# Two more queues in program order, and fillers in alternate units, in the attention of an encoder kernel

## The chip, the cores and the metric

The kernel runs on one core of a Trainium2 chip. The time is device microseconds of one execution. A core has engines that run side by side, each with its own in-order instruction queue: TensorE (PE, with its weight loads shown as PEld), VectorE (DVE), ScalarE (ACT), GpSimd (POOL) and SyncE (SP). In this kernel SP issues only DMA transfers, and POOL issues DMA transfers besides its elementwise work. An instruction waits on its queue until what it needs is done, and what stands behind it on that queue waits too.

## The reference, cut to what matters

The input x is 4 batches of 2048 tokens of 256 features, all in float32. The first part of the network is a dense attention with 16 heads of 16 features, a prior added to the scores and a residual:

```python
x = x + attn(layernorm(x))          # this part is "the attention" below
x = x + ffn(layernorm(x))           # two layers of local attention and gated MLP

def attn(x):
    Q, K, V = heads(x @ Wq.T + bq), heads(x @ Wk.T + bk), heads(x @ Wv.T + bv)
    scores = Q @ K^T / sqrt(16) + prior_lambda * gaussian_mask
    out = softmax(scores) @ V
    return merge(out) @ Wo.T + bo
```

For each of 64 pairs of batch and head, a 2048 x 2048 matrix of scores is made, its row maxima are taken, it is exponentiated and multiplied with V. The second part has two layers; its code is called "the local layers" here.

## The kernel before, in words

**Units.** The attention is one loop over t (line 1062 and on in the kernel before), from 0 to 1047. A unit u is 128 tokens of one head, so 16 units make a head, 256 a batch, 1024 the whole. Each turn of the loop does a first pass on unit t and a second pass on unit t − 20 (`LEAD` = 20). The first pass computes the scores of 128 queries against all keys and takes their row maxima (four products, line L775, read by DVE in L787, L789 and L799 and by ACT in L795). The second pass computes the scores again, transposed, with the negative row maxima as extra rows of the operand (four products, L858), adds the prior in the diagonal band (DVE, L869), exponentiates (ACT, L873) and multiplies with V (eight products, L882).

**The row of maxima.** At the end of a head, `negated` (L803 and on) turns its maxima into a row on DVE (L807 to L818). SP stores the row to DRAM (L820) and loads it back, rearranged, into the operand `q2` of the second pass (L824). The second pass of that head needs it about three units later, at units 4, 20, 36 and so on. SP also loads the pieces of q and k for both passes (L708), which are due some units later.

**Fillers.** The rest of the attention is cut into generators, which a timetable runs between the steps of the loop, in two slots per unit (`fill`, called at steps F and E). A filler that wants a product on PE asks `on_pe` first, which lets one filler product through per unit:

```python
def on_pe():
    while phase["at"] is not None and (phase["at"] or phase["taken"]):
        yield 1
    phase["taken"] = True
```

The fillers are: `projections(b)`, which normalises x of the next batch (`normed`, which loads x on POOL's queue) and computes q, k, v of it, with sends from SP to DRAM (L577) of parts made on POOL (L583, L584); `prepare_layers`, which splits the weights and tables of the local layers (loads and stores by SP, L239; POOL's work at L253, L255 and L317); and `residual(b)`. The projections of batch b start 60 units (`PROJECT_AT`) into batch b − 1; the residual of batch b starts 23 units into batch b + 1.

**The residual.** `residual(b)` transposes the attention's output (`oT`, eight fillers), and then goes through four groups g of 512 tokens. For each group, `fetch(g)` loads x (L453) and adds bo to it on POOL (L928); two products with Wo follow (`ao`), which DVE adds to x (L978); the sum is stored (L982); then its statistics are taken on DVE (bn_stats, L987), one of four per unit, with `var` and `nmean` (L991, L994); POOL computes `rstd` (L992) and the normalised `f` (four operations, L1003) and stores it (L1007). For batches 0 to 2, `fetch(0)` stands before the loop and `fetch(g)` at the head of group g; all these DMAs are on POOL's queue. For the last batch, at the end of attention, they are on SP's queue, and `fetch(g + 2)` stands at the end of group g.

**The order.** The attention is written out in the order in which it is to run, and a `manual_schedule` block makes PE, ACT and DVE take that order. In the kernel before, SP and POOL are not in that set: their queues are put in order by a scheduler, apart from the instructions wrapped in `keep_in_program_order`. The local layers follow after the attention with an order of their own, which the change does not touch.

## Time and profile before

| | |
|---|---|
| time, median of 3 | 5775.2 us (5774.78 to 5780.23) |
| the profiled execution | 5777.33 us, of which the span of the profile 5775.5 us |
| PE, DVE, ACT, POOL busy | 5472.3, 4821.5, 4477.9, 2187.8 us |
| mean granted TensorE clock | 0.985 of full |
| attention | from 78 to 3091 us; the last residual to about 3125 us |
| local layers | from there to the end |

The page shows the span in 40 slices with each engine's busy share in tenths, and the clock that TensorE was granted:

```profile
PE   5999999999999999999997899999999999999998
PEld 3444444444444444444444787888787788888787
DVE  5888999879998789999995888888888788888886
ACT  1888998879988799989996677667666666667765
POOL 2232112331012300010002565666665666666665
PEclk7999999999999999999998999999999999999999
```

A slice is 144 us. The attention is the first 21 slices and some, the local layers the rest; between them one slice is less busy. Names such as L775 are lines of the kernel; `s<-k,q` names what an instruction writes and reads. A bracket such as `[4.52 <-DMA x<-in_x]` is idle time of the engine ahead of the instruction, and what ended it. SPq is SP's queue, where only issuing is seen.

### The profile page before, as it was taken

What the parts mean: (1) busy time and instruction counts of PE and PEld (TensorE: products, weight loads), DVE (VectorE), ACT (ScalarE), POOL (GpSimd) and SP (SyncE); (2) the same over time, 40 slices, a digit from 0 to 9 for tenths busy, and PEclk for the clock granted to TensorE, in tenths of its full rate; (3) what the DMA queues carried; (4) which work ended last, traced back from release to release, by engine and by line L of the source; (5) the groups of instructions that cost most, each with busy time, mean ns of one, the idle gap of its engine ahead of it and who ended that gap; (6) DMA issues with size and microseconds to landing.
All of it is one profiled execution on the core that took longest, in us unless ns stands there. A gap on an engine that the chain in (4) does not pass through costs nothing.

```text
span 5775.5 us, 105276 instructions
## 1 busy us (share of the span) xinstructions
PE 5472.3 (95%) x35544; PEld 3386.2 (59%) x35544; DVE 4821.5 (83%) x13779; ACT 4477.9 (78%) x9384; POOL 2187.8 (38%) x2364
## 2 busy tenths in 40 slices
PE   5999999999999999999997899999999999999998
PEld 3444444444444444444444787888787788888787
DVE  5888999879998789999995888888888788888886
ACT  1888998879988799989996677667666666667765
POOL 2232112331012300010002565666665666666665
PEclk7999999999999999999998999999999999999999
DMA  4454234442234522232213212221223222222221
GB/s 128 144 163 118 80 101 135 149 132 82 74 90 123 156 71 62 76 100 61 61 54 110 51 48 55 51 55 51 56 51 84 82 62 58 60 60 55 64 53 40
DMA packets 336841, 477.29 MB, mean 83 GB/s; under 512 B 67376, under 2 KB 191280, under 8 KB 334768
## 3 DMA queue, kind: packets, MB, share of 16 engines
q1 hardware_dynamic: 322480, 432.79, 25.9%
q0 software_dynamic: 13824, 37.78, 2.3%
q8 instruction: 284, 4.65, 0.3%
q14 instruction: 253, 2.07, 0.1%
HBM read 268.79 MB, written 126.09 MB: 68 GB/s over the span
## 4 chain that ended last, share of the span: by engine, by line
PE 56%; DVE 23%; ACT 9%; POOL 6%; issue 3%; DMA 3%; SPq 0%; POOLq 0%; DVEq 0%; ACTq 0%
PE s L775 16%; PE acc L882 15%; PE s L858 8%; PE w L407 4%; ACT sim L1353 4%; PE sim L1327 3%; POOL rn L376 3%; DVE s L789 3%; PE qkv L407 2%; DVE lk L1189 2%; PE po L1407 2%; DVE sim L1339 2%; DVE tops L787 2%; DVE hn L1472 2%; DVE lq L1189 1%
## 5 line engine op out<-in xcount | busy, mean ns | idle before, releaser
L873 ACT ACTIVATE e<-s 128x512 f32<-128x512 f32 x4096 | 2157.9, 614 | 197.9 <-PE s L858 138.4
L775 PE MATMUL s<-k,q 64*128 64x512 f32 x3200 | 1294.7, 467 | 74.3 <-DMA q<-sm 27.2
L789 DVE CUSTOM_DVE_ANT_0 s<-s,wide 128x512 f32<-128x512 f32 x1408 | 973.3, 694 | 185.5 <-PE s L775 175.1
L882 PE MATMUL acc<-e,v 128*32 128x512 f32 x8192 | 1094.2, 606 | 0.3
L858 PE MATMUL s<-q,k 64*128 64x512 f32 x4096 | 841.7, 418 | 29.4 <-DMA q<-rowd 12.6
L775 PEld LDWEIGHTS s<-k,q 64*128 64x128 f32 x3200 | 535.6, 186 | 522.0 <-ACT more L795 257.6
L1353 ACT ACTIVATE sim<-sim,top,rn 128x256 f32<-128x256 f32 (+1 forms) x1024 | 600.6, 590 | 261.3 <-DVE top L1345 253.1
L787 DVE TENSOR_REDUCE tops<-s 128x1 f32<-128x512 f32 x896 | 611.9, 683 | 80.8 <-PE s L775 74.1
L1364 POOL TENSOR_TENSOR sim<-sim,inv 128x512 f32<-128x512 f32 (+1 forms) x512 | 512.8, 1022 | 347.9 <-DVE inv L1361 347.8
L858 PEld LDWEIGHTS s<-q,k 64*128 64x128 f32 x4096 | 542.3, 186 | 163.8 <-ACT e L873 57.3
L795 ACT ACTIVATE more<-s 128x512 f32<-128x512 f32 x896 | 541.3, 604 | 116.9 <-PE s L775 84.0
L799 DVE CUSTOM_DVE_ANT_0 more<-s,more 128x512 f32<-128x512 f32 x896 | 614.0, 685 | 0.0
L775 PEld LDWEIGHTS s<-kd,q 64*128 64x128 f32 x896 | 165.5, 185 | 743.9 <-DVE tops L789 382.6
L869 DVE TENSOR_TENSOR s<-s,band 128x187 f32<-128x187 f32 (+2 forms) x1408 | 474.7, 355 | 90.2 <-PE s L858 89.7
L407 PE MATMUL w<-gt,ww 128*128 128x512 f32 x2112 | 544.9, 397 | 3.5 <-DVE lk L1189 3.1
L775 PE MATMUL s<-kd,q 64*128 64x512 f32 x896 | 447.1, 499 | 1.2 <-DVE tops L787 0.5
L407 PEld LDWEIGHTS w<-gt,ww 128*128 128x128 f32 x2112 | 386.9, 189 | 79.1 <-issue 3.7
L1339 DVE CUSTOM_DVE_ANT_0 sim<-sim,cst 128x256 f32<-128x256 f32 (+1 forms) x1024 | 376.6, 409 | 57.5 <-PE sim L1327 54.0
L1252 POOL TENSOR_TENSOR r<-r,t 128x256 f32<-128x256 f32 x512 | 366.8, 737 | 149.7 <-DVE t L1239 140.0
L376 POOL TENSOR_TENSOR rn<-ss,nhalf 128x16 f32<-128x16 f32 x128 | 372.7, 2912 | 96.5 <-DVE ss L375 93.6
L1327 PE MATMUL sim<-lk,lq 128*128 128x256 f32 (+1 forms) x2048 | 340.8, 296 | 27.7 <-DVE lq L1189 19.1
L1386 PE MATMUL pT<-cst,sim 128*128 128x128 f32 x1984 | 280.7, 278 | 75.4 <-DVE lk L1189 34.2
(173 smaller groups left out, 9416.5 us busy)
## 6 DMA issues: line engine op xcount, KB each, us to landing
lk<-lk SPq DMA_DIRECT2D x256, 256.0 KB
sm<-part SPq DMA_DIRECT2D x192, 256.0 KB
q<-sm SPq DMA_DIRECT2D x512, 96.0 KB
k<-sm SPq DMA_DIRECT2D x512, 96.0 KB
k<-sm SPq DMA_DIRECT2D x128, 192.0 KB
q<-sm SPq DMA_DIRECT2D x128, 192.0 KB
fg<-f SPq DMA_DIRECT2D x32, 512.0 KB
tb<-td SPq DMA_DIRECT2D x128, 128.0 KB
```

The costliest lines, as they stand in the source:

```text
L376: nc.gpsimd.tensor_tensor(dst, var, nhalf[:, : var.shape[1]], ALU.pow)
L407: nc.tensor.matmul(ps, a, c, start=first and k == 0 and i == 0, stop=last and k == n - 1 and i == 2,)
L775: nc.tensor.matmul(ps, q1[u // 4 % Q_BUFS][rows, u % 4 * P : (u % 4 + 1) * P], keys, start=True, stop=True,)
L787: nc.vector.tensor_reduce(top, ps, AX.X, ALU.max)
L789: nc.vector.tensor_tensor_reduce(ps, ps, prior, 1.0, LOWEST, ALU.add, ALU.max, top)
L795: nc.scalar.activation(more, pairs.pop((u, 1, half)), AF.Relu)
L799: nc.vector.tensor_tensor_reduce(more, ps, more, 1.0, LOWEST, ALU.add, ALU.max, tops[u // NC][:, chunk(u), 2 * half : 2 * half + 1],)
L858: nc.tensor.matmul(ps, k2[s // 4 % Q_BUFS][rows, kc % 4 * P : (kc % 4 + 1) * P], q2[h % 2][rows, j % 2 * QT : (j % 2 + 1) * QT], start=Tru ...
L873: nc.scalar.activation(e, sums.pop((s, j)), AF.Exp)
L882: nc.tensor.matmul(acc[32 * j : 32 * j + 32, :], vs[b, kc][:, own * VS : own * VS + 32], es_.pop((s, j)), start=kc == 0, stop=kc == NC - 1,)
L1327: nc.tensor.matmul(ps[:, par, :width], q[:, par, pair, :], kst[:, par, part, windows, pair, :], start=part == 0, stop=part == 1,)
L1353: nc.scalar.activation(w, w, AF.Exp, bias=m["top"][:, h : h + 1], scale=s["rn"][:, h : h + 1], accum_out=m["sums"][:, h : h + 1],)
```

## The change

Three things change, all in the attention.

1. The `manual_schedule` block names all five engines, so SP's and POOL's queues are also in the order in which the program is written. The `keep_in_program_order` wrappers on the way, which then say nothing new, are removed.
2. `fill` marks PE as taken in every odd unit after `LEAD`, so a filler product is let through in even units only, one in two units.
3. `PROJECT_AT` goes from 60 to 90: the projections of batch b start 30 units later in batch b − 1.

Each engine executes the same instructions as before. With fillers in alternate units, the projections of a batch take about 100 units (units 90 to 196 of the batch before) where they took 68 (60 to 127), and a group of the residual takes 8 units where it took 6.

```diff
+ALL_ENGINES = tuple(
+    getattr(mybir.EngineType, name) for name in ("PE", "Activation", "DVE", "Pool", "SP")
+)
...
-PROJECT_AT, STRIDE, XT_BUFS = 60, 1, 4
+PROJECT_AT, STRIDE, XT_BUFS = 90, 1, 4
...
         def load(dst, src):
-            tc.keep_in_program_order(nc.sync.dma_start(dst, src))
+            nc.sync.dma_start(dst, src)
...
-            tc.keep_in_program_order(nc.gpsimd.tensor_copy(h, s))
-            tc.keep_in_program_order(
-                nc.gpsimd.tensor_tensor(low, s, h.bitcast(F32), ALU.subtract)
-            )
+            nc.gpsimd.tensor_copy(h, s)
+            nc.gpsimd.tensor_tensor(low, s, h.bitcast(F32), ALU.subtract)
...
                 def fetch(g):
                     t = x1s_[g] = load_x(b, g, queue, apart_by_four)
-                    tc.keep_in_program_order(
-                        nc.gpsimd.tensor_tensor(
-                            t, t, bo_sb.unsqueeze(1).to_broadcast([P, 4, D]), ALU.add
-                        )
+                    nc.gpsimd.tensor_tensor(
+                        t, t, bo_sb.unsqueeze(1).to_broadcast([P, 4, D]), ALU.add
                     )
...
             def fill(t, at):
-                phase["at"], phase["taken"] = at, False
+
+                phase["at"], phase["taken"] = at, t > LEAD and t % 2 == 1
                 fillers.run(2 * t + at + 1)

-            es.enter_context(tc.manual_schedule(engines={mybir.EngineType.PE, mybir.EngineType.Activation, mybir.EngineType.DVE}))
+            es.enter_context(tc.manual_schedule(engines=set(ALL_ENGINES)))
             for t in range(total + LEAD + 4):
```

The wrapper around the table products of `prepare_layers` (L317) goes in the same way.

More of the change, by code (lines that the diff above doesn't have):

```diff
@@ L315, in prepare_layers @@
                         cols = slice(h * half, (h + 1) * half)
-                        tc.keep_in_program_order(
-                            nc.gpsimd.tensor_tensor(
-                                tb[:, :, i : i + 2, cols], rot[:, :, i : i + 2, :],
-                                sc[:, i // 2, cols].unsqueeze(1).unsqueeze(1).to_broadcast(
-                                    [P, 2, 2, half]
-                                ),
-                                ALU.mult,
-                            )
+                        nc.gpsimd.tensor_tensor(
+                            tb[:, :, i : i + 2, cols], rot[:, :, i : i + 2, :],
+                            sc[:, i // 2, cols].unsqueeze(1).unsqueeze(1).to_broadcast(
+                                [P, 2, 2, half]
+                            ),
+                            ALU.mult,
                         )
@@ L926, in fetch @@
                     t = x1s_[g] = load_x(b, g, queue, apart_by_four)
-                    tc.keep_in_program_order(
-                        nc.gpsimd.tensor_tensor(
-                            t, t, bo_sb.unsqueeze(1).to_broadcast([P, 4, D]), ALU.add
-                        )
+                    nc.gpsimd.tensor_tensor(
+                        t, t, bo_sb.unsqueeze(1).to_broadcast([P, 4, D]), ALU.add
                     )
```

## The prediction

> **What bounds the kernel now.** I read the page's busy rows first, then the busy time by window, then the excess of each attention unit over a plain one, and last the chain and the queues where that excess sits. TensorE bounds everything:

> ```profile
> PE 5472.3 (95%) x35544; PEld 3386.2 (59%) x35544; DVE 4821.5 (83%) x13779; ACT 4477.9 (78%) x9384; POOL 2187.8 (38%) x2364
> ```

> In the windows below, the columns after start and end are the length, then busy us and instructions of PE, PEld, DVE, ACT and POOL, the clock, the DMA share and GB/s:

> ```profile
> 1500.00:1700.00 200.00, 198.62 (x1223) 83.31 (x1216) 182.94 (x539) 187.40 (x367) 4.14 (x10) 1.00 0.25 72
> 2700.00:2900.00 200.00, 198.48 (x1216) 82.08 (x1214) 183.40 (x549) 191.06 (x375) 4.00 (x10) 1.00 0.22 63
> 1253.00:1273.00 20.00, 11.83 (x60) 4.79 (x56) 9.12 (x28) 9.45 (x20) 0.76 (x11) 0.74 0.49 148
> 2005.00:2025.00 20.00, 7.98 (x48) 3.83 (x48) 6.50 (x20) 7.42 (x16) 3.81 (x6) 0.71 0.73 213
> ```

> The first window is an undisturbed stretch of attention: PE busy 198.6 of 200 us. A unit issues 16 products without fillers, so 1216 of them are 76 units, 2.63 us each with the end of each head in it (2.60 to 2.61 without). There, only less PE work or nothing at all can help. The two 20 us windows differ: PE stands 8.2 and 12.0 us. Stepping through the starts of all units, I find such holes at four: unit 124 (473 us, 5.1 us over a plain unit and its filler), 132 (502 us, 4.6), 388 (1256 us, 10.2) and 644 (2010 us, 13.6), together 33.5 us. The nine `ao` units of three residuals that follow a normalisation are 0.96 to 1.23 long, 9.6 in all. Unit 21 is 3.4 long (147 us), in the fill of the pipeline, and I leave it alone. The rest of the excess is some 0.5 to 0.75 per head, ordinary work.

> The third hole, on SP's timeline (start, length, engine, line, operation):

> ```profile
> 1252.84 0.40 SPq L708 DMA_DIRECT2D k<-sm  x1
> 1253.34 0.40 SPq L675 DMA_DIRECT2D sv<-vst  x1
> 1253.83 3.75 SPq L708 DMA_DIRECT2D q<-sm  x2
> 1257.63 1.39 SPq L708 DMA_DIRECT2D k<-sm  x3
> 1259.14 0.35 SPq L820 DMA_DIRECT2D rowd<-row  x1
> 1262.38 1.32 SPq L824 DMA_DIRECT2D q<-rowd  x2
> ```

> and in the chain of waits of the same stretch (start, length, what):

> ```profile
> 1257.00 7.53 issue
> ```

> The first score product of a head's second pass needs its row of maxima (L820 out, L824 back in). DVE had that row at about 1248; SP sends it at 1259.14, behind pieces of k and q and a store of v that nobody needed soon. PE starts 2.15 after L824 began, at 1264.53. At 2010 the same place is `q<-rowd` at 2017.39, behind a copy of local-layer weights; at 502 the row store at 498.48; at 473 POOL itself stood 4.44 on `s_rot` ahead of `full` and `part`.

> **The change part by part.** All durations are from the profiled execution: span 5775.5, run 5777.3, 2.1 above the median of 5775.2. I make the sum against 5777.3 and take 2.1 off at the end. Every engine keeps the same instructions; only order and waits move.

> *The four holes, −33.5.* With SP in program order the row store comes right after the negated maxima, ahead of the head's k and kd loads; the only things before it at 388 are three sends of a `part` that POOL was given two units (5.2 us) earlier. The route of a row takes 5.4 us (1259.14 to 1264.53) and the program leaves three units and more, 8 to 9 us. Weight copies of the local layers move to their own place behind attention, and POOL's wait on `s_rot` comes three slots later by the program's own spacing. Ends: 0 if SP's new waits delay the row as much, −33.5; I take the whole, because the route has 3 us to spare.

> *The residual's x, +48.6 +6 −9.6.* This is the cost I see. Before, the scheduler pulled the load of x for the next group forward on POOL's queue, where it could:

> ```profile
> 947.45 1.04 POOL L992 TENSOR_TENSOR rstd_f<-var_f,nhalf 128x4 f32<-128x4 f32 x1 [8.71 <-DVE nmeanf L994]
> 948.61 2.17 POOL L1003 TENSOR_SCALAR f<-x,nmeanf,rstd_f 128x256 f32<-128x256 f32 x4
> 951.07 0.82 POOL L1007 DMA_DIRECT2D f<-f  x1 [0.30 <-POOL f L1003]
> 951.89 0.77 POOL L453 DMA_DIRECT2D x<-in_x  x1
> 957.17 2.38 POOL L928 TENSOR_TENSOR x<-x,bo_sb 128x1024 f32<-128x1024 f32 x1 [4.52 <-DMA x<-in_x]
> ```

> Here L453 fetches a group ahead of its use (the sum L978 of that group ran at about 967). In program order, `fetch(g)` for g = 1, 2, 3 stands behind group g−1's `rstd_f`, four `f` and the store of `f`, and DVE's sum L978 of the same group g stands two units after `nmeanf` of g−1. From the end of `nmeanf` (947.44) to the end of L928 (959.55) is 12.1 us on POOL and its queue. Before, `nmeanf` to the next L978 was 3.1 us (950.54) at one unit's distance; one unit more makes 5.7. So L978 waits 6.4, and behind it on DVE stand all maxima and band sums of the unit, and behind those PE, which owns three banks for the first products. I take 1.0 off for what PE can do meanwhile: 5.4 for each of nine (three groups, batches 0 to 2), 48.6. Ends: the x loads landed in 4.2 to 8.5 us (median 5.3); the fast end with 2.0 off for a PE lead gives 3.3 each, 30; the slow end gives 9.6 each, 86. The middle follows the row that shows this very load. Group 0's load comes behind the last oT, with 0.8 issue, 5.3 landing and 2.4 for L928, 8.5 in all, against about 5.5 until its L978: 2 each after the same discount, 6 for three (ends 0 and 15). The 9.6 of the `ao` units are the present end of this very path and lie inside these stalls, so they come off.

> The trace has this wait once already, at the end of attention, where a load was fetched as late:

> ```profile
> 3114.27 1.28 DVE L978 TENSOR_TENSOR x<-x,ao 128x512 f32<-128x512 f32 x2 [6.77 <-POOL x L928]
> ```

> [...] The measured row is 5.3 us from issue to landing for 512 KB. [...]

> *The projections' x, +3.* Their load is followed by two units until bn_stats, about 6.5 us with a filler; issue 0.8 and landing 5.3 make 6.1. POOL is nearly idle (4 of 200 us) and may be early. Twelve loads: ends 0, and 2 each or 25 with slow landings; near the low end as the median fits.

> *The passage to the local layers, +5.* There SP issues the batch-3 loads, and in program order the load of group 2 follows the store of `f` of group 0 and of group 1's sum, group 3's that of group 1's `f`. Before, the last load left at 3116.60 and PE then stood 15.52 for L978. I put it some 4 to 7 later; ends 0 and +10.

> *Fillers in every other unit, 0.* A filler product costs PE its own length (q/k product 1.30 over a plain unit, `ao` 1.32, transposes 0.72) wherever it stands, as PE is full in plain units. Cover: ACT (191 of 200) and DVE (183) get 1.3 us of PE time to do the evacuation. Ends −4 and +5, from the 0.35 per bn_stats unit that the residual and projections have now.

> *Projections from unit 90, 0.* They then end at about 196 of 256; the next batch's first keys and rows are fetched some 20 units before 256, so 40 units (104 us) remain. If that cover failed, PE would stand for what is missing.

> *Waits that stay.* SP waits 821.5 us for PE before L708 and POOL 891.6 before the memset L767; in program order the things behind them are due later, so I price these at nothing.

> Sum: 5777.3 −33.5 +48.6 +6 −9.6 +3 +5 = 5796.8, less 2.1: **5795 us**.

> **Rivals.**
> 1. *The x loads stay hidden* (ends faster). PE's lead in PSUM or an early POOL covers the nine stalls. For it: the forecast turns at 3.2 us per load (33.5+9.6−6−3−5 over nine), close to my low end of 3.3. Against it: the 6.77 wait above. With none of them: 5775.2 −33.5 +5 = 5747.
> 2. *Slow landings.* Loads meet sends and weight loads, 8.5 instead of 5.3: 3.2 more each, 29 on nine: 5824. The DMA share in the residual's window is 0.55 against 0.22 in quiet ones, which speaks for some of it.
> 3. *The row stalls come back.* A send that waits for POOL blocks SP, and the row store behind it: nothing of the 33.5 is won, 5828. Against: the send's `part` is two units old.
> 4. *The two sides cancel*, each x stall near 3: within 0.2% of before, which is 11.5 us and about what a measurement of this kernel can tell from no change.

> **How the numbers follow.** Forecast with stalls of 3.5 to 7.5 each 0.57 (own range 5778 to 5814); hidden 0.20 (5747 to 5765); slow landings 0.10; row stalls back 0.08; cancelled 0.05. The range leaves out the lowest and highest tenth: 5752 to 5826. Faster 0.20 from the hidden case; same 0.12, from the cancelled case and the forecast's low edge; slower 0.68.

> **What the changed profile would show.** Right: SP's L820 within 1 us of the row at every head, no 7 us "issue" in the chain, and the holes at 1256 and 2010 gone; in its place DVE's sum of x and `ao` waiting for POOL's sum of x and bo, nine times 5 to 7 us in three groups, with POOL waiting for x behind the store of `f`; PE short by the same time in those windows. Wrong: few such waits, or these waits with PE still busy; or rows still late.

## The result and the profile after

The changed kernel takes 5873.5 us (median of 4, 5871.7 to 5876.1) against 5777.7 for the kernel before (median of 4): a ratio of 1.0166, 95% interval 1.0148 to 1.0183, 96 us slower. I forecast slower, but 5795 and no more than 5826.

Line numbers of the kernel after are two to four lower in the attention: L775 is L773, L858 is L856, L882 is L880, L978 is L974, L928 is L925, L453 is L451, L820 is L818. First the page's busy times, then windows of 20 and more us (start and end, length, busy us and instructions of PE, PEld, DVE, ACT and POOL, the clock, the DMA share, GB/s), all of the kernel after:

```profile
PE 5494.3 (94%) x35544; PEld 3400.0 (58%) x35544; DVE 4822.1 (82%) x13779; ACT 4470.8 (76%) x9384; POOL 2184.9 (37%) x2364
```

```profile
1255.00:1275.00 20.00, 20.00 (x126) 9.42 (x126) 15.44 (x47) 17.14 (x35) 4.56 (x9) 1.00 0.72 210
980.00:1000.00 20.00, 13.87 (x79) 7.44 (x77) 9.86 (x28) 7.94 (x15) 4.80 (x5) 0.74 0.38 116
2060.00:2085.00 25.00, 15.06 (x80) 6.16 (x79) 12.59 (x42) 12.07 (x25) 4.60 (x7) 0.74 0.38 106
```

The stretch around 1256, where PE stood 8 us before, is now full: 20.00 of 20. At each of the 64 heads SP now sends the row of maxima (L818) 0.03 us after DVE has it; before, the worst row, ready at 1249.20, left 9.94 us later. New holes stand at 980 to 1000 (a residual) and at 2060 to 2085 (projections). PE's busy time rose by 22 us with the same number of instructions, so some of its products became slower.

The waits, sorted, say the same (engine, what waited, for what: us in total, times, longest):

```profile
PEld s L773 <- DVE tops L787: 517.8, 615, 10.7
DVE x L974 <- POOL x L925: 101.7, 14, 9.1
POOL x L925 <- DMA x<-in_x: 76.8, 14, 9.4
```

In the kernel before, DVE waited for that sum of POOL twice, 12.6 us in all, both behind the attention.

**The balance.** I stepped through the starts of all 1024 units in both traces and took off a plain unit (2.605 us) and the fillers' products; "excess" below is what is left of a unit. The spans differ by 95.2 us (5870.7 − 5775.5):

| | us |
|---|---|
| first 20 units, the filling of the pipeline (unit 20 starts at 138.3, was 144.8) | −6.5 |
| the four row holes (units 124, 132, 388, 644) | −33.5 |
| nine waits for x in groups 1 to 3 of the residuals, 7.6 to 9.4 each | +75.5 |
| three waits for x in group 0, 5.4 to 5.9 each | +16.8 |
| projections: units 140 to 142, 193, 401 to 402, 653 to 654 | +31.8 |
| from the last unit to the first qkv of the local layers (88.9, was 80.3) | +8.6 |
| local layers (2650.1 both) | 0 |
| small differences in the other units | +2.5 |

One wait of the residual, on three engines of the kernel after; first POOL:

```profile
976.61 1.04 POOL L988 TENSOR_TENSOR rstd_f<-var_f,nhalf 128x4 f32<-128x4 f32 x1 [8.79 <-DVE nmeanf L990]
977.77 2.16 POOL L999 TENSOR_SCALAR f<-x,nmeanf,rstd_f 128x256 f32<-128x256 f32 x4
980.23 0.82 POOL L1003 DMA_DIRECT2D f<-f  x1 [0.30 <-POOL f L999]
981.05 0.77 POOL L451 DMA_DIRECT2D x<-in_x  x1
986.48 2.34 POOL L925 TENSOR_TENSOR x<-x,bo_sb 128x1024 f32<-128x1024 f32 x1 [4.67 <-DMA x<-in_x]
```

then DVE, whose sum stands on the queue ahead of the next maxima:

```profile
988.85 0.69 DVE L974 TENSOR_TENSOR x<-x,ao 128x512 f32<-128x512 f32 x1 [6.74 <-POOL x L925]
```

then PE:

```profile
982.99 1.06 PE L880 MATMUL acc<-e,v 128*32 128x512 f32 x8
983.99 0.49 PE L773 MATMUL s<-kd,q 64*128 64x512 f32 x1
990.62 0.79 PE L773 MATMUL s<-k,q 64*128 64x512 f32 x1 [6.13 <-DVE tops L785]
990.62 1.64 PE L856 MATMUL s<-q,k 64*128 64x512 f32 x4
992.61 1.93 PE L880 MATMUL acc<-e,v 128*32 128x512 f32 x8
```

This is the step the prediction described: the load of x behind `rstd`, `f` and the store of `f`, 12.2 us from the end of DVE's `nmeanf` to the end of the sum with bo; DVE waits 6.74; PE has 0.6 us of lead and waits 6.13. What it lacked is in the last two rows: after the wait, four L856 take 1.64 us and eight L880 take 1.93, against 1.06 for the eight before it. The granted clock of that window is 0.74; it is 0.50 from 986.76 to 997.00 and 1.00 around that.

A wait of the projections, POOL first and then DVE:

```profile
2066.05 0.61 POOL L581 CAST partd<-full 128x512 fp32r<-128x512 f32 x1 [8.84 <-DMA sd<-partd]
2066.74 1.28 POOL L582 TENSOR_TENSOR partd<-full,partd 128x512 fp32r<-128x512 f32 x1
2067.95 1.21 POOL L575 DMA_DIRECT2D sd<-partd  x2
2069.59 0.60 POOL L575 DMA_DIRECT2D sd<-partd  x1 [0.43 <-issue]
2070.17 0.82 POOL L451 DMA_DIRECT2D x<-in_x  x1
```

```profile
2077.41 0.43 DVE L538 BATCH_NORM_STATS2 st_a<-x 128x6 f32<-128x256 f32 x1 [10.85 <-DMA x<-in_x]
```

The x load of the next projection group stands behind the differences of keys. The second of these needs a `part` buffer that the first store must release, so POOL waits 8.84 us for that DMA; the load goes out only then, and bn_stats waits 10.85 us with everything of DVE behind it.

### The profile page after: what moved, and what is told of

It reads as the page before. It is cut to its first block, busy times and chain, and to the rows that moved or that the text cites. A ratio compares the mean times of both kernels' runs of the same rounds, so it can differ in the third digit from the quotient of the medians.

```text
span 5870.7 us, 105058 instructions
## 1 busy us (share of the span) xinstructions
PE 5494.3 (94%) x35544; PEld 3400.0 (58%) x35544; DVE 4822.1 (82%) x13779; ACT 4470.8 (76%) x9384; POOL 2184.9 (37%) x2364
## 4 chain that ended last, share of the span: by engine, by line
PE 23%; DVE 16%; ACT 8%; POOL 5%; issue 2%; DMA 1%; POOLq 0%; DVEq 0%; SPq 0%; ACTq 0%
PE w L405 4%; ACT sim L1350 4%; PE acc L880 3%; PE s L773 3%; PE sim L1324 3%; POOL rn L374 3%; PE qkv L405 2%; DVE lk L1186 2%; DVE sim L1336 2%; PE po L1404 2%; PE s L856 2%; DVE hn L1469 2%; DVE lq L1186 1%; PE pT L1383 1%; ACT lk L1302 1%
## 5 line engine op out<-in xcount | busy, mean ns | idle before, releaser
L773 PE MATMUL s<-k,q 64*128 64x512 f32 x3200 | 1299.1, 471 | 141.9 <-DVE tops L787 52.2
L880 PE MATMUL acc<-e,v 128*32 128x512 f32 x8192 | 1106.9, 612 | 0.6
L856 PE MATMUL s<-q,k 64*128 64x512 f32 x4096 | 868.0, 423 | 11.6 <-DVE xT L570 4.7
L773 PEld LDWEIGHTS s<-k,q 64*128 64x128 f32 x3200 | 540.8, 187 | 565.3 <-ACT more L793 236.6
L856 PEld LDWEIGHTS s<-q,k 64*128 64x128 f32 x4096 | 549.0, 188 | 161.0 <-ACT e L871 58.7
L773 PEld LDWEIGHTS s<-kd,q 64*128 64x128 f32 x896 | 166.4, 186 | 772.0 <-DVE tops L787 413.3
L405 PE MATMUL w<-gt,ww 128*128 128x512 f32 x2112 | 545.2, 397 | 3.5 <-DVE lk L1186 3.1
L911 POOL TENSOR_TENSOR oall<-o,inv 128x256 f32<-128x256 f32 x64 | 39.8, 623 | 1265.1 <-DVE inv L910 1096.7
L773 PE MATMUL s<-kd,q 64*128 64x512 f32 x896 | 450.4, 503 | 18.5 <-DVE tops L787 13.6
L405 PEld LDWEIGHTS w<-gt,ww 128*128 128x128 f32 x2112 | 387.3, 189 | 79.2 <-issue 3.7
L1324 PE MATMUL sim<-lk,lq 128*128 128x256 f32 (+1 forms) x2048 | 341.0, 296 | 25.6 <-DVE lq L1186 18.7
```

Of the source, the lines that this page charges most:

```text
L405: nc.tensor.matmul(ps, a, c, start=first and k == 0 and i == 0, stop=last and k == n - 1 and i == 2,)
L773: nc.tensor.matmul(ps, q1[u // 4 % Q_BUFS][rows, u % 4 * P : (u % 4 + 1) * P], keys, start=True, stop=True,)
L856: nc.tensor.matmul(ps, k2[s // 4 % Q_BUFS][rows, kc % 4 * P : (kc % 4 + 1) * P], q2[h % 2][rows, j % 2 * QT : (j % 2 + 1) * QT], start=Tru ...
L880: nc.tensor.matmul(acc[32 * j : 32 * j + 32, :], vs[b, kc][:, own * VS : own * VS + 32], es_.pop((s, j)), start=kc == 0, stop=kc == NC - 1,)
L1324: nc.tensor.matmul(ps[:, par, :width], q[:, par, pair, :], kst[:, par, part, windows, pair, :], start=part == 0, stop=part == 1,)
```

## The experiments

Theory A: the loss comes from POOL's queue in program order, which puts the x loads late; B: from the spacing and start of the fillers; C: from SP's order. The first four runs undo or do single parts.

**All five queues in order, nothing else of the change:**

```diff
-PROJECT_AT, STRIDE, XT_BUFS = 90, 1, 4
+PROJECT_AT, STRIDE, XT_BUFS = 60, 1, 4
-phase["at"], phase["taken"] = at, t > LEAD and t % 2 == 1
+phase["at"], phase["taken"] = at, False
```

> The kernel after with a filler product in every unit again and the projections at 60 again: all five queues in program order is the only thing left of the change. Theory A (program order on POOL puts each residual's x load behind the f of the group before, and each projection's x load behind the store of the key differences): the holes stay, and those of the residual are longer, since a group has one unit less between nmeanf and the sum L974: 9 us of DVE wait instead of 6.7 to 8.8 at nine places, so about 5890 us (5865 to 5920). Theory B (the spacing and the later start of the fillers cost the time): the cost is gone and the four row holes too, about 5740 us.

Measured: 5891.0 us, ratio 1.0201 (1.0186 to 1.0216). B is out. The waits of DVE for x are fewer and longer, as expected with one unit less between:

```profile
DVE x L974 <- POOL x L925: 114.6, 11, 11.7
```

One row hole is still there in this run: unit 644 is 16.7 us over a plain one. SP waits at the weight load that the run with SP alone shows below.

**The spacing and the start alone, in the kernel before:**

```diff
-PROJECT_AT, STRIDE, XT_BUFS = 60, 1, 4
+PROJECT_AT, STRIDE, XT_BUFS = 90, 1, 4
-phase["at"], phase["taken"] = at, False
+phase["at"], phase["taken"] = at, t > LEAD and t % 2 == 1
```

> The kernel before with fillers in alternate units and the projections at 90, SP and POOL still ordered by the scheduler. Theory A: no wait of DVE for POOL's sum of x and bo inside the attention; within 20 us of before (5755 to 5795), the row holes possibly at other units. Theory B: about 5870 us.

Measured: 5748.5 us, ratio 0.9955 (0.9940 to 0.9970). These two parts win 27 us by themselves, more than A allowed for: the holes over 2 us that are not in the filling of the pipeline come to 17 us (units 36, 196, 452, 708) in place of 33.5, and the 24 `ao` units of three residuals, together 10.4 us over a plain unit and its filler before, are 2.0 over.

**SP alone in program order, and POOL alone, each in the kernel before:**

```diff
-engines={mybir.EngineType.PE, mybir.EngineType.Activation, mybir.EngineType.DVE}
+engines={mybir.EngineType.PE, mybir.EngineType.Activation, mybir.EngineType.DVE, mybir.EngineType.SP}
```

The other kernel has `Pool` in place of `SP`.

> The kernel before with SP's queue also in program order, POOL's by the scheduler. Theory A: the row holes at units 132, 388 and 644 go, no x waits come: 5740 to 5755 us. Theory C (SP's waits in program order hold the rows and sends up): above before, up to 5870.

> The kernel before with POOL's queue also in program order, SP's by the scheduler. Theory A: all x waits of the changed kernel, at before's spacing, on top of most of the row holes: 5880 to 5930 us. Theory C: within 15 us of before.

Measured: 5760.7 with SP (0.9972, 0.9962 to 0.9981) and 5882.5 with POOL (1.0195, 1.0176 to 1.0213). C is out, and POOL's order alone accounts for the loss. SP's order wins 15 us and not 20 to 35, because the hole at unit 644 stayed, and at 19.4 us was larger than before's. SP's timeline there, and SP's wait:

```profile
1971.81 2.41 SPq L1148 DMA_DIRECT2D wq<-q  x1
1994.00 0.33 SPq L1148 DMA_DIRECT2D wk<-k  x1
1994.43 0.38 SPq L1148 DMA_DIRECT2D wv<-v  x1
1994.90 0.38 SPq L820 DMA_DIRECT2D rowd<-row  x1
```

```profile
SPq L1148 <- DMA sd<-partd: 19.4, 1, 19.4
```

The row of maxima was ready on DVE at 1979.15. SP stood at a weight load of the local layers, which waited 19.4 us for a store of key differences, and the row behind it. That load is not written in the attention, and the order of the attention doesn't hold it. In the kernel after, it goes at 2227 and blocks nothing.

**The loads earlier.** If A holds, moving the x loads up in the changed program must return the time. In the residual:

```diff
-                    elif not last and g:
-                        fetch(g)
...
                     queue.dma_start(apart_by_four(x1s[b], g), x1)
+                    if not last and g < 3:
+                        fetch(g + 1)
```

> The kernel after, with the fetch of group g+1 moved ahead of the statistics of group g (right behind the store of x1), so that it stands before rstd, f and the store of f on POOL's queue. Theory A: the twelve waits of DVE for POOL's sum of x and bo shrink to the three of group 0; the nine others cost 8.3 to 10.5 us of PE each in the changed kernel, about 76 in all: near 5797 us. If instead the landing itself is late (transfers contending), waits of 4 us or more stay and the time is above 5830.

In the projections, the load of group g + 1 goes behind the normalisation of group g:

```diff
-                xt = load_x(b, g) if b else x_first[:, 4 * g : 4 * g + 4]
                 if b:
-                    for _ in range(4):
-                        yield
+                    if g == 0:
+                        early[b, 0] = load_x(b, 0)
+                        for _ in range(4):
+                            yield
+                    xt = early.pop((b, g))
+                else:
+                    xt = x_first[:, 4 * g : 4 * g + 4]
...
                         xt[:, i], xt[:, i], neg[:, i : i + 1], rstd[:, i : i + 1], ALU.add, ALU.mult
                     )
+                if b and g < 3:
+                    early[b, g + 1] = load_x(b, g + 1)
```

> The kernel after, with the x load of a projection group g+1 moved up behind the normalisation of group g, so that it stands before the differences and their store on POOL's queue. Theory A: the waits of bn_stats for x (22.1 us in four) and the holes at units 140 to 142, 193, 401 and 653 go, 31.8 us together: near 5842 us. If they come from the key differences' store itself, they stay and the time is near 5870.

> Both moves together, all else as in the kernel after. Theory A: the two savings add, 5873 less 76 and 32: about 5765 us, so that the program order of both queues pays once the loads stand early enough; 5755 to 5780. If the holes only give way to others, above 5800.

Measured: 5792.3 (1.0029, 1.0017 to 1.0041), 5837.4 (1.0114, 1.0097 to 1.0131), and both together 5757.6 (0.9972, 0.9961 to 0.9983). The savings, 81 and 36 us, add to 117; together they are 116. All three came out 5 to 7 us below the expected number. In the residual those 5 us are the `ao` units right behind the nine holes, which went too (point 4 below).

**The two places left.** Group 0's x is fetched ahead of the eight `oT` fillers; for the last batch, bo is added when a group begins. `fetch` now only issues the load, and `add_bo` is the addition on POOL, which for batches 0 to 2 still follows each load:

```diff
                 oTs = []
+                fetch(0)
+                if not last:
+                    add_bo(0)
                 for n in range(8):
...
-                fetch(0)
                 for g in range(4):
                     if last and g == 0:
                         fetch(1)
+                    if last:
+                        add_bo(g)
```

> Both early moves, and the two places left: group 0's x is fetched ahead of the eight oT fillers, and for the last batch bo is added when a group begins and not when its load is issued, so that rstd and f of the group between don't wait behind a load on POOL. Theory A: the three waits of group 0 (5.0 to 5.8 us of PE each, 16 in all) go, and the passage to the local layers, 88.8 us from the last unit to the first qkv, comes back to before's 80: 5757.6 less 16 and 8, about 5734 us (5727 to 5745). If only one of the two was rightly placed, 5742 to 5750.

Measured: 5738.7 us, ratio 0.9935 (0.9920 to 0.9950): 0.65% faster than the kernel before. Three waits of 5 us in group 0 are gone, and the passage to the local layers is 80.4 us again.

**The change without POOL.** Spacing, start and SP's order, with POOL left to the scheduler:

```diff
-engines={mybir.EngineType.PE, mybir.EngineType.Activation, mybir.EngineType.DVE}
+engines={mybir.EngineType.PE, mybir.EngineType.Activation, mybir.EngineType.DVE, mybir.EngineType.SP}
```

(in the kernel with the spacing and the start, above)

> Fillers in alternate units and projections at 90, SP in program order, POOL by the scheduler: the change without POOL. Theory A (all of the loss is POOL's order): faster than both the spacing alone (5748.5) and SP alone (5760.7), about 5735 us, 5728 to 5748. If SP's order costs something once the fillers are spread, 5750 or more.

Measured: 5738.6 us, ratio 0.9936 (0.9921 to 0.9950). This is the same time as the hand-ordered POOL queue with its loads moved up: on the changed program, POOL's order cost 135 us, and with its loads moved up it won nothing. PE's busy time is 5459.4 us, 13 less than before.

**Spacing and start apart**, each alone in the kernel before:

```diff
-phase["at"], phase["taken"] = at, False
+phase["at"], phase["taken"] = at, t > LEAD and t % 2 == 1
```

> The kernel before with fillers in alternate units alone, projections at 60. The spacing and the start together won 27 us. If the spacing does it (a send, a row and loads find SP's queue and the transfers less crowded), about 5750 us; if the start does it, about 5775.

```diff
-PROJECT_AT, STRIDE, XT_BUFS = 60, 1, 4
+PROJECT_AT, STRIDE, XT_BUFS = 90, 1, 4
```

> The kernel before with the projections at 90 alone, a filler in every unit. If the spacing is what won, the holes only move to other units: about 5775 us, 5765 to 5785. If the start does it, about 5750.

Measured: 5768.1 (0.9986, 0.9976 to 0.9996) and 5765.2 (0.9979, 0.9969 to 0.9988). Neither expectation holds well: alone they win 10 and 13 us, and both together 27; the second time lies on the edge of the range for holes that only move. Each alone has holes, only elsewhere: with the spacing alone at eleven units between 36 and 676, some 36 us together, so that its win lies in the `ao` units and in the start of the attention; with the start alone at units 164 (8.0), 420 (6.3) and 676 (11.3), 25.6 us together. Why the scheduler leaves 17 us of holes with both and more with one stays open; it was not tried further.

**The price of a hole.** To part the wait from what follows it, the waits of groups 1 to 3 are shortened, not removed: the load goes out right after `rstd`, ahead of `f` and its store, and bo is added behind that store.

```diff
-                    t = x1s_[g] = load_x(b, g, queue, apart_by_four)
+                    x1s_[g] = load_x(b, g, queue, apart_by_four)
+                    if last or g == 0:
+                        add_bo(g)
...
-                    elif not last and g:
-                        fetch(g)
...
                     if not last:
                         yield
+                        if g < 3:
+                            fetch(g + 1)
                     for i in range(4):
...
                     queue.dma_start(apart_by_four(fs[0][b], g), f)
+                    if not last and g < 3:
+                        add_bo(g + 1)
```

> The kernel after, with the load of x for the next group issued right after rstd and ahead of the four f and their store, and bo added behind that store: the nine waits of groups 1 to 3 are shortened, not taken away. From rstd's end the load takes 0.8 plus about 5.4 and the sum 2.3, so DVE waits 3.2 to 3.4 us less at each of the nine (6.6 to 8.8 become 3.3 to 5.5). Theory A, waits alone: nine times 3.3, about 5844 us. [...]

Measured: 5820.8 us (5814.2 to 5833.1), ratio 1.0083 (1.0066 to 1.0100), 53 us less than the kernel after and more than the 30 expected: DVE's waits for x fell by 36.4 us (101.7 to 65.3), 4.0 for each of nine and not 3.3, and that is not all of it. The trace is that of the fastest execution, 5814.2. Two holes on PE in it, a short one and a long one:

```profile
1043.46 0.50 PE L773 MATMUL s<-k,q 64*128 64x512 f32 x1 [1.76 <-DVE tops L785]
1043.46 0.96 PE L856 MATMUL s<-q,k 64*128 64x512 f32 x4
1044.58 1.06 PE L880 MATMUL acc<-e,v 128*32 128x512 f32 x8
```

```profile
1014.76 0.79 PE L773 MATMUL s<-k,q 64*128 64x512 f32 x1 [4.35 <-DVE tops L787]
1014.77 1.64 PE L856 MATMUL s<-q,k 64*128 64x512 f32 x4
1016.77 1.94 PE L880 MATMUL acc<-e,v 128*32 128x512 f32 x8
```

After the wait of 1.76 us the products have their full speed; after that of 4.35 they take 1.7 and 1.8 times as long, until about 4 us later. Five of the six short holes cost 1.7 to 1.8 us, the wait and nothing more; the three long ones 5.6 to 6.1, their wait of 4.1 to 4.4 and 1.5 to 1.8 besides. So a long hole costs more than its wait. The sixth short hole, at 1752.93, cost 3.3:

```profile
1752.93 0.71 PE L773 MATMUL s<-k,q 64*128 64x512 f32 x1 [1.73 <-DVE tops L785]
1752.93 1.56 PE L856 MATMUL s<-q,k 64*128 64x512 f32 x4
1754.85 1.84 PE L880 MATMUL acc<-e,v 128*32 128x512 f32 x8
```

So 1.7 us can bring the slow products or not. The windows of the same run around the sixth short hole, and around the short one shown first, tell the two apart (columns as above; the clock stands ahead of the DMA share):

```profile
1749.64:1753.05 3.41, 1.68 (x13) 0.46 (x13) 1.88 (x6) 1.84 (x4) 1.58 (x2) 1.00 0.26 90
1753.05:1756.46 3.41, 3.41 (x15) 1.26 (x15) 2.89 (x9) 2.34 (x5) 0.00 (x0) 0.50 0.03 5
1039.66:1043.08 3.42, 2.04 (x13) 0.52 (x13) 1.39 (x5) 1.40 (x3) 2.09 (x2) 1.00 0.39 137
1043.08:1046.49 3.41, 3.03 (x20) 1.39 (x20) 3.38 (x11) 3.17 (x7) 0.00 (x0) 1.00 0.03 5
```

In every trace of this case the granted clock is 1.00 or 0.50 and changes only at times that lie whole steps of 3.413 us apart (to 0.004 us), and each of these windows is one such step. The wait that ends at 1752.93 lies within one step, PE is busy for 1.68 of its 3.41 us, and the next step has half the clock. The wait that ends at 1043.46 is cut by the border at 1043.08 into 1.38 and 0.38, and the clock stays full. The other four short waits are cut in the same way, with at most 1.54 us of idle PE in one step. In the fourteen traces together, from 150 to 3040 us, 11,636 steps have the full clock: none of the 11,479 with under 0.8 us of idle PE was followed by half the clock, all 90 with 1.8 us or more were, and of the 67 between 15 were. So in these traces the half clock went with how much of one step PE had stood idle, and a wait of 1.7 us brought the slow products or not by where it fell.

## Why the prediction was wrong

The direction held and so did the mechanism: POOL's order made the x loads late, DVE stood at its sum, and PE behind it. The row holes went to the last of the 33.5 us, though at unit 644 with some luck. The prediction had the weight loads of the local layers move behind the attention. The load that stood ahead of the row there (L1148, L1145 in the kernel after) still goes inside it, and in the two runs with SP in order and the projections from 60 it brought a hole at that unit of 16.7 and 19.4 us. With the projections from 90 it goes at 2227 and meets no row. Three terms were mis-sized, and a fourth had the wrong cause.

1. **The nine waits, +48.6.** They cost 75.5. Term by term: the DVE wait, put at 6.4, was 7.5 on average (6.6 to 8.8; in group 2 the normalisation of a head's output, L911, stands between `rstd` and `f` and waits for DVE, which is about 1 us of the 2 more). The discount of 1.0 for PE's lead was right: PE waited 6.7, 0.9 less. The step that failed is what a PE wait costs: I counted the wait alone, and the products after it ran at half the clock, 1.7 us more in the unit of each hole. Twelve residual holes at 1.7 are 21 us, and 8 more stand in the units behind them (point 4). The trace of before had this in sight: the windows I quoted at the two large holes show a clock of 0.74 and 0.71, and I read only their busy time.

   In the runs every gap of 3.6 us and more brought slow products, and so did some shorter ones: one gap of 1.73 us of six, and in the kernel after one of 2.13 (at 664.68), which was followed by eight L880 in 1.89.

2. **Group 0, +6.** It was 16.8. I put DVE's wait at 3 and it was 5.0 to 5.6, and PE's waits of 3.6 to 4.2 brought the slow products too (eight L880 in 1.93 behind each).

3. **The projections' x, +3, with 25 as its far end.** These units were 31.8 over. In 24.8 of that DVE waits for x: units 141 and 142, 401 and 402, 653 and 654, with waits of 6.26, 4.33 and 10.85. The rest is something else: 4.1 at unit 140, where a filler's product waits 2.52 for a weight load on SP's queue (`s_w<-in_l_w`), and 3.0 at unit 193, where one cast on DVE (L810) takes 2.18 and not 0.17; why it does stays open.

   Two steps failed in the term. I took POOL as nearly idle and therefore early. It is idle because it waits: the differences stand ahead of the load, and their second half waits for the first half's store to land, 7.30 ahead of unit 141 and 8.84 ahead of unit 653. The rows were there, `sd<-partd` with 7.9 us to landing on the page of before and POOL's wait of 9.17 for it at 2008. The rule I had followed for the residual, to list everything ahead of a load on its queue, I didn't follow here. And I took 5.3 for the landing. The twelve loads landed in 7.1 us in the median (4.7 before), and the one for unit 401 in 10.64, with no wait of POOL at those differences. Issued ahead of the differences' stores, the nine moved loads landed in 3.8 to 4.3.

4. **The `ao` units, −9.6.** I took these to be the present end of the same path, a late x. They were not. In the kernel before, DVE's sum waits there 0.57 to 1.04 us and starts within 0.1 of the end of the `ao` product; in the first residual x with bo had been ready for 8 us and more at each of the three.

   ```profile
   950.54 0.69 DVE L978 TENSOR_TENSOR x<-x,ao 128x512 f32<-128x512 f32 x1 [0.57 <-PE ao L407]
   ```

   The spacing alone took this excess off (10.4 us to 2.0 over the 24 units), with no wait for x in its place. In the kernel after, the `ao` units are 10.1 us over again. Now 8.3 of it stand in the twelve right behind the holes, where the clock can still be half (0.50 to 997.00 in the hole shown above): the products below took 1.69 in the unit ahead of the hole.

   ```profile
   995.63 2.29 PE L405 MATMUL ao<-aw,oT 128*128 128x256 f32 x12
   ```

5. **The passage, +5,** was 8.6, within its ends. **Fillers and start, 0 each:** alone they win 27 us under the scheduler, so 0 was wrong there; what they do once the queues are in order is smaller: 17 us between the run with the order alone (5891) and the kernel after, with 13 us less of DVE waiting for x (114.6 against 101.7) and without the hole of 16.7 at unit 644. The start of the attention, which I left out, gave 6.5.

The rivals: the hidden loads and the cancelling case are refuted by 101.7 us of waits. The slow landings did not happen at the nine loads (5.3 to 5.4, one 6.9); they did in the projections (point 3). The returned row holes did not come in the kernel after; one did in the two runs named above. The range ended at 5826 because its terms were added near their middles; even with the far ends of the x terms and of the passage together it would have ended at 5868.

## What to carry to other kernels

Before putting a queue into program order, list for every load on it what stands ahead and what that waits for; a load that a scheduler had pulled forward must be pulled forward by hand, and then the order may pay (5738.7 here with the loads moved, 5873.5 without). Price a stall of the bounding TensorE by its length, and add a slow restart: here it cost 1.5 to 2.9 us, always after waits of 3.6 us and more, and after shorter ones by how much of the wait fell into one step of the clock (in these traces always from 1.8 us of 3.41 on). A queue that is idle because it waits is not a queue that runs early.

## What was not expected of the hardware

The slow restart of TensorE. In 11 of 12 residual holes of the kernel after, with PE waits of 3.6 to 7.7 us, the eight L880 that follow take 1.93 to 1.94 us in place of 1.06, and in one 1.69; it made no difference whether the wait was 3.62 or 7.35. In the unit of the hole the loss is thus a step of 1.5 to 1.8 us that doesn't grow with the wait. The unit behind it loses 0.03 to 1.16 more, since half the clock lasts to the end of a step, 3.3 to 6.5 us after PE resumed: 1.5 to 2.9 in all, and 29 us for the twelve, beside 71.5 of waiting. Waits of 1.7 to 1.8 us brought it in one case of six, the one that lay within a single step of 3.413 us.
